# One run of context products per block, beside the 13th of fifteen tiled products, in a two-layer graph-attention kernel

## The chip, the cores and the metric

The kernel runs on one core of a Trainium2 chip. The metric is the device time of one execution in microseconds (us), the median of three. TensorE (PE in the profile; PEld for its weight loads) multiplies, VectorE (DVE), ScalarE (ACT) and GpSimd (POOL) work on tiles, SyncE (SP) issues the transfers. All data is fp32.

## The reference, cut to what matters

There are 128 batches of 64 rows by 768 features, with an adjacency matrix each. The input is normalised and clipped at zero, then two layers follow, and the input is added to their result:

```
m_left, m_right = h @ W_left[l].T, h @ W_right[l].T
u_left, u_right = h @ m_left^T / sqrt(768), h @ m_right^T / sqrt(768)
u   = u_left on and above the diagonal of adj, u_right below it
att = exp(u) * adj / sum over the row
ctx = att @ (h @ W_lin[l].T + b_lin[l])
h   = relu((ctx - mean) / (std + 0.001) * a + b)
```

Here `std` is the deviation with 767 in the divisor. `ctx` is the context.

## The kernel before, in words

**Tiling.** The batches are cut into 16 blocks of 512 rows (`NB = 16`, `T = 512`). Each layer has two passes over the blocks. `pass_one` normalises and transposes the rows, projects them with W_left and then W_right (`project`), and makes the attention (`scores` and a chain of small operations). `pass_two` multiplies with W_lin (`linear`), multiplies with the attention (`context`), and normalises (`finish`). `ps_aux` is two tiles of two PSUM banks each; the four other banks are called X, Y, Z and V.

**Fifteen tiled products.** A 768-wide projection is not done in plain form. It is a bilinear scheme over tiles of 2x128 by 256: 15 products (the list `ORDER`) of sums of weight tiles (`W_SUMS`, on slots named by numbers) with sums of token tiles (`T_SUMS`, tiles `ts`; `B0` to `B5` are raw tiles of `ht`). Each product accumulates into X, Y, Z or V, and after it the bank is read into the result `hl` or `m` with the signs in `ORDER`'s last column (`read`). The first read of a result is an ACT copy (L200), the later ones are DVE additions (L155). A bank is not cleared between most products: the next product in the same bank adds on top, so it may start only when all reads of the product before it in that bank are done. `FIRST` lists the six products that begin a bank anew; `fresh` then fills the bank with a bias on ACT (L605). In index order the banks are X Z X Y X V X Y X V X Y V Z V. The reads after products 0, 2, 4, 6 and 7 are on ACT alone, product 1 has one on each engine, and all others are on DVE; products 8 and 10 have two.

**Order.** Nothing is scheduled by a planner: every engine runs its instructions in the order in which the program writes them. `put(slot, f)` hangs extra work into a block: slot 2i is in the middle of product i, slot 2i+1 behind it and behind its reads. What stands at slot 30 or more when a block ends is carried into the next block with 30 taken off. `idle` holds work without a slot.

**Context and finish.** In `pass_two` the context of block u-1 is made inside block u in two halves, r = 0 after product 0 and r = 1 after product 7 (`ends`). A half is eight matmuls of 64 rows by 64 columns with 384 elements each, over four quadrants of the array, into the two `ps_aux` tiles (L636). `finish` then squares and sums on ACT (L705, L707), takes the inverse on DVE (L710, L711) and scales (`scaled`). In layer 0 the scaling is an ACT copy (L723) and the rows go to DRAM. In layer 1 it is a DVE operation that reads PSUM (L715), then POOL adds the offset row (L718), then DVE adds the residual row from SBUF (`done`, L730) and the result is stored:

```
nc.gpsimd.tensor_add(zs[k], zs[k], rows["b"])
nc.vector.scalar_tensor_tensor(xs[k], zs[k], 0.0, xs[k], op0=ALU.max, op1=ALU.add)
```

The last block of each layer is done in two half-width runs.

**Start.** The first block's rows and the weights of layer 0 are loaded raw, and the weight sums are made by POOL and DVE while the first products run. `hold` makes POOL wait for a tile, so that its sums start late enough. `needs` says which sums DVE makes ahead of which product.

Of the kernel before, what the change touches and what calls it, by code (L numbers as in the profile page):

```python
# [10 lines left out]
F32 = mybir.dt.float32  # L11
# [6 lines left out]
def kernel(  # L18
# [68 lines left out]
    def run(slot):  # L87
# [3 lines left out]
        elif idle:  # L91
            f = idle.popleft()
            if f is not None:
# [3 lines left out]
    SRC = {"l": w_left, "r": w_right, "n": w_lin}  # L97
    RAW = {9: (2, 1), 8: (0, 1), 13: (2, 0), 12: (1, 1), 3: (0, 2), 10: (1, 2), 11: (0, 0), 6: (1, 0), 14: (2, 2)}
    W_SUMS = ((9, "+", 9, 8), (5, "+", 8, 13), (8, "+", 8, 12), (0, "+", 8, 13), (4, "+", 3, 10),
              (11, "+", 11, 13), (1, "+", 4, 11), (7, "+", 6, 10), (6, "-", 12, 6), (12, "-", 14, 12),  # L100
              (12, "-", 12, 9), (6, "+", 6, 5), (2, "-", 9, 14), (10, "-", 14, 10), (10, "-", 10, 9),
              (3, "+", 3, 11), (7, "+", 7, 3))
# [5 lines left out]

    ORDER = ((8, "X", "ta", "+2"), (5, "Z", "u1", "-0+2"), (0, "X", "u2", "+3"), (1, "Y", "u3", "-3"),
             (12, "X", "B3", "-5"), (6, "V", "B0", "-2"), (2, "X", "td", "-4"), (4, "Y", "tb", "+1"),  # L110
             (10, "X", "B4", "+0-2"), (7, "V", "B1", "+3"), (3, "X", "u0", "+1-3"), (11, "Y", "te", "+0"),
             (13, "V", "tc", "-1"), (9, "Z", "tg", "+4"), (14, "V", "tf", "+5"))
    FIRST = {0: ("X", 8), 1: ("Z", 5), 3: ("Y", 1), 5: ("V", 6), 9: ("V", 7), 12: ("V", 13)}
    W = {}
# [98 lines left out]

    ident = const.tile([P, P], F32, name="ident")
    make_identity(nc, ident)
    eps_in = const.tile([P, 1], F32, name="eps_in")
# [3 lines left out]

    diff = const.tile([P, S], I32, name="diff")
    tri = const.tile([P, 2, S], F32, name="tri")
    for h in range(PAIR):
        r = slice(h * S, (h + 1) * S)
        nc.gpsimd.iota(diff[r], pattern=[[-1, S]], base=0, channel_multiplier=1)
    nc.vector.tensor_scalar(tri[:, 0, :], diff, 0.0, None, op0=ALU.is_le)
    nc.vector.tensor_scalar(tri[:, 1, :], diff, 0.0, None, op0=ALU.is_gt)
    def mean_var(mv, halves):
        st = stat.tile([P, 2, 6], F32, name="st")
        for n in range(2):  # L230
            nc.vector.bn_stats(st[:, n, :], halves[n])
        nc.vector.bn_aggr(mv, st)


    XR, KEEP = {}, {}

# [35 lines left out]
    def transpose_rows(l, u, pool):  # L272
# [58 lines left out]
        if (l, u) == (0, 0):  # L331
            ht = HT[key] = big.tile([P, C, T], F32, name="ht")

            def turn(n, q):

                if n < 2:
                    p = ps_aux.tile([P, 2, T], F32, name="aux")
                    banks = [p[:, 0], p[:, 1]]
                else:
                    banks = [ps_st.tile([P, 2 * TH], F32, name=m) for m in ("XY", "ZV")[n - 2]]  # L340
                for m, p in enumerate(banks):
                    for c in range(3):
                        nc.tensor.transpose(p[:, c * P:(c + 1) * P],
                                            xr[q][:, (3 * m + c) * P:(3 * m + c + 1) * P], ident)
                for m, p in enumerate(banks):
                    to = ht[:, 3 * m:3 * m + 3].rearrange("p c (a g s) -> p g c a s", a=4, g=2)
                    to = to[:, q // 2, :, q % 2 * 2:q % 2 * 2 + 2, :]
                    (nc.vector.tensor_copy if n < 2 else nc.scalar.copy)(
                        to, p[:, :3 * P].rearrange("p (c a s) -> p c a s", c=3, a=2))
# [28 lines left out]
    def pass_one(l, aside):  # L378
        with tc.tile_pool(name=f"one{l}", bufs=2, reuse_waits="tile") as sp:
# [110 lines left out]
            just = {}  # L490
            if l == 0:
                load_rows(0, 0, sp)
                warm = stat.tile([P, 1], F32, name="warm", bufs=1)
                nc.scalar.activation(warm, eps_in, AF.Sqrt)
                for f in load_w(0, "l") + load_w(0, "r"):
                    f()
# [14 lines left out]
                hold(KEEP["nb"][:, START[-1]:START[-1] + 1])  # L511
                for f in ws[:3]:
                    f()
                t, w = deque(sums_t((1, 0, 0), nc.vector)), deque([vs[4], vs[3]] + vs[5:])
                needs = ("tw", "wt", "t", "ttww", "wwww", "w", "tw", "t", "ww", "ww", "", "t", "t", "t", "t")
                for i, what in enumerate(needs):
# [14 lines left out]
            for u in range(NB):  # L531
                slot = 0
                if u == 0:
                    if l == 0:
                        rs = sums_w(0, "r", nc.gpsimd)
                        put(16, lambda: hold(M[0][:, 0, 4, 0, :1]))
                        for n in range(0, len(rs), 3):
                            put(17 + n // 3, *rs[n:n + 3])
                    slot = 14 if l else 15
# [69 lines left out]
    def pass_two(l, aside):  # L609
        last = l == L - 1  # L610
        with tc.tile_pool(name=f"two{l}", bufs=2, reuse_waits="tile") as sp:
# [3 lines left out]
            else:  # L615
                places(sp, {"hl": ([P, Q, H], 2), "at": ([P, Q, S], 3), "x": ([P, 2, H], 2),
                            "xb": ([P, H // 32, Q, 32], 1), "z": ([P, H], 3)}, ("hl", "at", "x", "xb", "z"))
            AT, HL = {}, {}

            def load(u):  # L620
                if (2, l, u) not in HT:
                    load_h(2, l, u)
                AT[u] = sp.tile([P, Q, S], F32, name="at", bufs=3)
                nc.sync.dma_start(AT[u], ATT[l][u])

            def context(u, r):
# [5 lines left out]
                for n in range(2):  # L632
                    for (j, k, i) in ((lo, 0, lo), (hi, 0, hi), (lo, 1, hi), (hi, 1, lo)):
# [3 lines left out]
                                         start=True, stop=True)  # L637
                return [c[:, :, :HH] for c in cx]

            def batch(r, k, h):  # L640
# [23 lines left out]
            def finish_last(u, r):  # L664
# [6 lines left out]
                xs = XS[u, r]  # L671
                ss = [stat.tile([P, 1], F32, name="ss_e", bufs=2) for _ in range(2)]
                rs = [stat.tile([P, 1], F32, name="sd_e", bufs=2) for _ in range(2)]
                for k in (1, 0):
# [13 lines left out]
            def residual(u, r):  # L688
                XS[u, r] = [sp.tile([P, H], F32, name="xr", bufs=4) for _ in range(2)]
                for k in range(2):  # L690
                    for h in range(PAIR):
                        nc.sync.dma_start(XS[u, r][k][h * S:(h + 1) * S], x[u * NBB + batch(r, k, h)])

            def finish(u, r):

                cx = context(u, r)
                zs = [sp.tile([P, H], F32, name="z", bufs=4 if last else 3) for _ in range(2)]
                if last and not u and not r:
                    residual(u, r)
                two = "p (n d) -> p n d"  # L700
                ss = stat.tile([P, 2], F32, name="ss")
                sd = stat.tile([P, 2], F32, name="sd1")
                rs = stat.tile([P, 2], F32, name="rs1")
                for k in range(2):
# [8 lines left out]
                def scaled(k):  # L713
# [8 lines left out]
                    else:  # L722
                        nc.scalar.activation(zs[k].rearrange(two, n=2), cx[k], AF.Copy, scale=rs[:, k:k + 1])  # L723
                    for h in range(PAIR):
                        nc.sync.dma_start(ROWS[u][batch(r, k, h)], zs[k][h * S:(h + 1) * S])

                def done(k):
                    if last:
                        xs = XS[u, r]
                        nc.vector.scalar_tensor_tensor(xs[k], zs[k], 0.0, xs[k], op0=ALU.max, op1=ALU.add)  # L730
                        for h in range(PAIR):
                            nc.sync.dma_start(out[u * NBB + batch(r, k, h)], xs[k][h * S:(h + 1) * S])
                        if k and u + r < NB - 1:
                            residual(u + r, 1 - r)

                return [inverse] + [lambda k=k: scaled(k) for k in range(2)] + [lambda k=k: done(k) for k in range(2)]

            def linear(u, rs, base, ends, more):
# [7 lines left out]
                for i, (s, at, t, _) in enumerate(ORDER):  # L746
# [12 lines left out]
                    if i in early:  # L759
                        bank[FIRST[early[i]][0]] = fresh(l, early[i], rs)  # L760
                    if i == 11 and more:
                        AHEAD.append(fresh(l, 0, more))
                    if i in ends:
                        what, slots = ends[i]
                        for f, n in zip(finish(*what), slots):
                            put(n, f)
                    run(base + 2 * i + 1)

            load(0)
            for u in range(NB):  # L770
                turn = not last and u >= NB - 2
                if u + 1 < NB:
                    load(u + 1)
                    put_all(9 if u else 15, affine(2, l, u + 1))
# [6 lines left out]
                    ends = {}  # L781
                    if u:
                        ends = {0: ((u - 1, 0), (6, 7, 8, 11, 12)), 7: ((u - 1, 1), (20, 21, 22, 30, 30))}
                    linear(u, (0, 1), 0, ends, (0, 1) if u + 2 < NB else (0,))
                    for n in sorted(plan):
                        plan[n - 30] = plan.pop(n)
                else:
                    if turn:
                        load_h(1, 1, 0)
                        put_all(28, affine(1, 1, 0), 3)  # L790
                        put_sums_t((1, 1, 0), 38, 2, 30)
                        ends = ({0: ((u - 1, 0), (12, 13, 15, 19, 21)), 11: ((u - 1, 1), (34, 35, 36, 42, 44))},
                                {4: ((u, 0), (50, 51, 52, 56, 58))})
                    else:
                        last_block(u)
                        ends = ({0: ((u - 1, 0), (12, 13, 15, 19, 21)), 9: ((u - 1, 1), (28, 29, 30, 39, 41))},
                                {2: ((u, 0), (44, 45, 47, 61, 62))})
                    linear(u, (0,), 0, ends[0], (1,))
# [53 lines left out]
```

## Time and profile before

| What | Before |
| --- | --- |
| time, median of 3 runs | 2761.18 us (2760.8 to 2761.21) |
| span of the profiled execution | 2761.9 us |
| PE busy | 2731.4 us, 99% |
| DVE busy | 1338.4 us, 48% |
| POOL busy | 1196.8 us, 43% |
| ACT busy | 842.5 us, 31% |
| transfers | 310.80 MB, mean 113 GB/s |
| TensorE clock granted | 0.999 |

A line of the timeline has the start, the duration, the engine, the source line, the operation, what it writes and reads, the shape and how many instructions are merged; in brackets stands how long the engine had been idle and who ended the wait. "issue" means that the profile shows nothing that was waited for. The kernel has two layers of about 55.7 us per block in the first pass and 29.2 us per block in the second.

### The profile page before, as it was taken

How to read it: one execution, taken by the hardware profiler on the slowest of the kernel's cores; microseconds unless marked ns; L12 is line 12 of the kernel's file. 1: busy time of each engine (PE TensorE's matmuls, PEld its weight loads, DVE VectorE, ACT ScalarE, POOL GpSimd, SP SyncE). 2: the span in 40 equal slices, each digit the busy share in tenths (PEclk: the TensorE clock that was granted, in tenths of full speed). 3: DMA queues.
4: the chain of work that ended last, by engine and by line, in shares of the span. 5: the costliest groups of instructions: out<-in, count | busy, mean ns of one | idle time of the engine just before them, and what ended most of it. 6: DMA issues, size and time to landing. Idle time of an engine off the chain costs nothing.

```text
span 2761.9 us, 46187 instructions
## 1 busy us (share of the span) xinstructions
PE 2731.4 (99%) x18712; PEld 2337.1 (85%) x18712; DVE 1338.4 (48%) x2250; ACT 842.5 (31%) x1469; POOL 1196.8 (43%) x940
## 2 busy tenths in 40 slices
PE   8999999999999999999999999999999999999998
PEld 6888888888888888888788888888888888888886
DVE  6555445545453332333335444444444335676667
ACT  3222223222321244444521211121121214444443
POOL 4332442223223465565432344223222325887885
PEclk9999999999999999999999999999999999999999
DMA  6423433343232343443555422443234204555655
GB/s 196 127 75 98 122 80 81 93 122 85 75 85 67 95 136 107 123 142 104 151 127 154 101 75 76 107 119 79 75 98 120 59 26 147 163 168 163 178 162 139
DMA packets 234068, 310.80 MB, mean 113 GB/s; under 512 B 54144, under 2 KB 184448, under 8 KB 225664
## 3 DMA queue, kind: packets, MB, share of 16 engines
q1 hardware_dynamic: 233696, 307.45, 40.4%
q8 instruction: 149, 2.44, 0.4%
q14 instruction: 63, 0.52, 0.1%
q10 hardware_dynamic: 160, 0.39, 0.0%
HBM read 202.91 MB, written 104.86 MB: 111 GB/s over the span
## 4 chain that ended last, share of the span: by engine, by line
PE 96%; DVE 2%; ACT 0%; issue 0%; DMA 0%; SPq 0%; DVEq 0%; ACTq 0%
PE X L422 24%; PE V L422 16%; PE Y L422 12%; PE X L752 12%; PE Z L422 8%; PE V L752 8%; PE Y L752 6%; PE aux L449 5%; PE Z L752 4%; PE aux L636 3%; DVE ts L155 0%; DVE wm L463 0%; DVE m L155 0%; DMA x<-in_x_dram 0%; DVE w_l L155 0%
## 5 line engine op out<-in xcount | busy, mean ns | idle before, releaser
L155 POOL TENSOR_TENSOR ts<-ht 128x512 f32<-128x512 f32 x441 | 585.6, 1339 | 1220.2 <-DMA ht<-h 531.5
L200 ACT ACTIVATE m<-X 128x512 f32<-128x512 f32 (+1 forms) x256 | 151.6, 592 | 1100.5 <-PE X L422 583.3
L155 POOL TENSOR_TENSOR ts<-ht,ts 128x512 f32<-128x512 f32 x189 | 249.1, 1325 | 151.0 <-PE X L752 75.9
L155 DVE TENSOR_TENSOR m<-m,V 128x512 f32<-128x512 f32 (+1 forms) x256 | 173.2, 677 | 269.6 <-PE V L422 269.5
L155 DVE TENSOR_TENSOR m<-m,X 128x512 f32<-128x512 f32 (+1 forms) x256 | 162.8, 677 | 249.1 <-PE X L422 248.4
L752 PE MATMUL X<-w_n,ts 128*128 128x256 f32 x1024 | 244.0, 380 | 1.3 <-DVE hl L155 0.7
L422 PE MATMUL X<-ts,w_l 128*128 128x256 f32 x1024 | 242.8, 380 | 1.7 <-POOL w_l L155 1.1
L422 PE MATMUL X<-ts,w_r 128*128 128x252 f32 (+1 forms) x1024 | 238.8, 376 | 0.0
L155 DVE TENSOR_TENSOR m<-m,Z 128x512 f32<-128x512 f32 (+1 forms) x128 | 87.4, 683 | 306.4 <-ACT m L200 247.3
L422 PEld LDWEIGHTS X<-ts,w_l 128*128 128x128 f32 x1024 | 192.0, 190 | 32.2 <-DVE m L155 2.7
L752 PEld LDWEIGHTS X<-w_n,ts 128*128 128x128 f32 x1024 | 191.6, 190 | 32.5 <-issue 2.1
L422 PEld LDWEIGHTS X<-ts,w_r 128*128 128x128 f32 x1024 | 192.0, 190 | 26.0
L268 ACT ACTIVATE ht<-ht,b_col,a_col 128x512 f32<-128x512 f32 x192 | 143.5, 804 | 133.4 <-DMA ht<-h 133.4
L752 PE MATMUL Y<-w_n,ts 128*128 128x256 f32 x768 | 182.5, 379 | 0.0
L422 PE MATMUL Y<-ts,w_l 128*128 128x256 f32 x768 | 181.4, 379 | 0.0
L200 ACT ACTIVATE hl<-X 128x512 f32<-128x512 f32 (+1 forms) x136 | 77.7, 571 | 333.2 <-PE X L752 330.2
L422 PE MATMUL Y<-ts,w_r 128*128 128x252 f32 (+1 forms) x768 | 179.1, 376 | 0.0
L752 PEld LDWEIGHTS Y<-w_n,ts 128*128 128x128 f32 x768 | 145.8, 190 | 20.4 <-issue 0.6
L422 PEld LDWEIGHTS Y<-ts,w_l 128*128 128x128 f32 x768 | 145.9, 190 | 19.8
L422 PEld LDWEIGHTS Y<-ts,w_r 128*128 128x128 f32 x768 | 145.9, 190 | 17.4
L155 DVE TENSOR_TENSOR hl<-hl,X 128x512 f32<-128x512 f32 (+1 forms) x136 | 83.0, 652 | 145.4 <-PE X L752 140.5
L155 DVE TENSOR_TENSOR hl<-hl,V 128x512 f32<-128x512 f32 (+1 forms) x136 | 89.0, 654 | 128.0 <-PE V L752 127.6
(142 smaller groups left out, 4711.4 us busy)
## 6 DMA issues: line engine op xcount, KB each, us to landing
ht<-h SPq DMA_DIRECT2D x63, 1536.0 KB, 7.3
h<-xb SPq DMA_DIRECT2D x124, 384.0 KB, 6.0
z<-z SPq DMA_DIRECT2D x128, 192.0 KB, 2.9
x<-z SPq DMA_DIRECT2D x128, 192.0 KB, 8.3
x<-in_x_dram SPq DMA_DIRECT2D x120, 192.0 KB, 8.5
xr<-in_x_dram SPq DMA_DIRECT2D x120, 192.0 KB, 3.6
out_dram<-xr SPq DMA_DIRECT2D x120, 192.0 KB, 2.6
adj<-in_adj_dram SPq DMA_DIRECT2D x64, 128.0 KB, 2.7
```

Of the source, the lines that this page charges most:

```text
L155: (eng.tensor_add if sign == "+" else eng.tensor_sub)(o, a, b)
L200: nc.scalar.activation(to(o), p, AF.Copy, scale=1.0 if sign == "+" else -1.0)
L268: nc.scalar.activation(ht, ht, AF.Relu, bias=cols[1][:, c:c + 1], scale=cols[0][:, c:c + 1])
L422: nc.tensor.matmul(p[:, g], w[ORDER[i][0]][:, c, g * P:(g + 1) * P], b()[t][:, c, :].rearrange(bs, s=S)[:, :, :ns], start=(new and g == c ...
L449: nc.tensor.matmul(p[h * S + e:h * S + e + 32, q, e:e + 95], ht[:, c, b * S + e:b * S + e + 32], mb[:, e:e + 95], start=(c == 0), stop=(c ...
L636: nc.tensor.matmul(cx[k][i, m, :HH], at[j, q, :], hl[j, q, m * HH:(m + 1) * HH], start=True, stop=True)
L752: nc.tensor.matmul(p[:, n], b[t][:, c, r * P:(r + 1) * P], w[s][:, c, :], start=(i in FIRST and i not in PRELOAD and n == c == 0), stop=(c ...
```

## The change

It moves the whole context of a block u-1 (u = 1 to 13) into one run of sixteen matmuls after product 12 of block u (`context_block`). The run needs six banks at once, so it takes both `ps_aux` tiles and the banks X and Y, which are then between their last read and the next block's first use. Each row of 768 is cut into 512 and 256 instead of 384 and 384. DVE copies the parts in X and Y to SBUF, so that the banks come free; squares, inverse, scaling and residual of all four tiles follow at fixed slots, the later ones in the next block (`finish_block`). Blocks 14 and 15 keep halves, at other products. Beside that:

- The two first products change places, and so do their weight sums, so that the first product needs one sum (slot 5 = 8 + 12). POOL makes two sums ahead instead of three.
- A tiny transfer that reads the first row tile is put ahead of the weight loads, so that these are issued after that tile has landed.
- The sums of W_right are held until the last token sum `tf`; four of them go from POOL to DVE.
- Attention tiles are loaded later, residual rows at fixed slots; constants that only the start needs move to a pool that is given back.

```diff
-    ORDER = ((8, "X", "ta", "+2"), (5, "Z", "u1", "-0+2"), (0, "X", "u2", "+3"), (1, "Y", "u3", "-3"),
+    ORDER = ((5, "X", "ta", "+2"), (8, "Z", "u1", "-0+2"), (0, "X", "u2", "+3"), (1, "Y", "u3", "-3"),
...
+                nc.sync.dma_start(dram.tile([1, 8], F32, name="first"), XR[0, 0][START[0]][:1, :8])
...
-                for f in ws[:3]:
+                for f in ws[:2]:
...
-                        put(16, lambda: hold(M[0][:, 0, 4, 0, :1]))
-                        for n in range(0, len(rs), 3):
-                            put(17 + n // 3, *rs[n:n + 3])
+                        put(24, lambda: hold(TS[1, 0, 0]["tf"][:, 0, :1]))
+                        put(25, *rs[:7])
+                        put_all(31, rv[7:11])
+                        put(35, *rs[11:14])
+                        put(36, *rs[14:])
...
+            def context_block(u):
...
+                aux = [ps_aux.tile([P, 2, T], F32, name="aux") for _ in range(2)]
+                x, y = (ps_st.tile([P, 2 * TH], F32, name=n) for n in "XY")
+                wide = {(1, 0): y, (1, 1): x, (0, 0): aux[0][:, 0], (0, 1): aux[0][:, 1]}
+                parts = {}
+                for r in (1, 0):
+                    for k in range(2):
+                        parts[r, k] = [wide[r, k], aux[1][:, k, r * D:(r + 1) * D]]
+                    rows_at = ((lo, 0, lo), (hi, 0, hi), (lo, 1, hi), (hi, 1, lo))
+                    first = [(j, k, i, int(j == hi)) for j, k, i in rows_at]
+                    then = [(j, k, i, int(j == lo)) for j, k, i in rows_at[1::2] + rows_at[::2]]
+                    for j, k, i, n in first + then:
+                        q = r + 2 * k
+                        nc.tensor.matmul(parts[r, k][n][i], at[j, q, :], hl[j, q, n * T:T + n * D],
+                                         start=True, stop=True)
...
+            def finish_block(u, more):
...
+                for t in ((1, 1), (1, 0)):
+                    nc.vector.tensor_copy(zs[t][:, cut[0]], parts[t][0])
+                    parts[t][0] = zs[t][:, cut[0]]
...
+                put_each((25, 26, 28, 29), squares)
+                put(30, deviation)
+                put(32, inverse)
+                put_each((33, 34, 35, 36), scaled)
+                if last:
+                    put_each((37, 39, 41, 43), lambda t: added_to(u, *t, zs[t]))
...
-                    if u:
-                        ends = {0: ((u - 1, 0), (6, 7, 8, 11, 12)), 7: ((u - 1, 1), (20, 21, 22, 30, 30))}
+                    if 0 < u < NB - 2:
+                        ends = {12: (u - 1, None)}
+                    elif u:
+                        ends = {5: ((u - 1, 0), (16, 17, 18, 24, 26)), 11: ((u - 1, 1), (28, 29, 30, 37, 39))}
...
-                        ends = ({0: ((u - 1, 0), (12, 13, 15, 19, 21)), 9: ((u - 1, 1), (28, 29, 30, 39, 41))},
-                                {2: ((u, 0), (44, 45, 47, 61, 62))})
+                        ends = ({1: ((u - 1, 0), (13, 14, 16, 20, 22)), 9: ((u - 1, 1), (28, 29, 30, 39, 41))},
+                                {2: ((u, 0), (44, 48, 51, 61, 62))})
```

## The prediction

> **What bounds the kernel now.** I read the page first (busy shares, chain that ended last), then the timeline of PE's weight loads in the second pass of layer 0, then the same stretch of layer 1 on all engines, then the start.
>
> ```profile
> PE 2731.4 (99%) x18712; PEld 2337.1 (85%) x18712; DVE 1338.4 (48%) x2250; ACT 842.5 (31%) x1469; POOL 1196.8 (43%) x940
> ...
> PE 96%; DVE 2%; ACT 0%; issue 0%; DMA 0%; SPq 0%; DVEq 0%; ACTq 0%
> ```
>
> PE never rests, so only two things can move the time: PE's own work, and new waits of PE. The weight loads show what a half context costs (layer 0):
>
> ```profile
> 1011.71 1.70 PEld L752 LDWEIGHTS Y<-w_n,ts 128*128 128x128 f32 x8
> 1013.75 0.21 PEld L636 LDWEIGHTS aux<-hl,at 64*64 64x64 f32 x8 [0.33 <-issue]
> 1014.12 0.15 PEld L636 LDWEIGHTS aux<-hl,at 64*64 64x64 f32 x4 [0.17 <-issue]
> 1014.45 0.15 PEld L636 LDWEIGHTS aux<-hl,at 64*64 64x64 f32 x4 [0.17 <-issue]
> 1015.20 1.59 PEld L752 LDWEIGHTS X<-w_n,ht 128*128 128x128 f32 x8 [0.60 <-issue]
> 1016.82 1.70 PEld L752 LDWEIGHTS V<-w_n,ht 128*128 128x128 f32 x8
> ```
>
> Products follow each other at 1.726 us (1020.27 to 1022.00 and on). Here Y to the context takes 2.04 (0.31 too much), the context 1.45, the next product 1.62 (0.10 less). A half costs 0.31 + 1.45 - 0.10 = 1.66, of which four waves of matmuls, 0.32 apart, are 1.28. So 0.37 is the price of going in and out. In layer 1 a block looks like this:
>
> ```profile
> 2491.17 1.94 DVE L715 SCALAR_TENSOR_TENSOR z<-aux,rs,a 128x768 f32<-128x768 f32 x2
> 2492.26 3.60 POOL L718 TENSOR_TENSOR z<-z,b 128x768 f32<-128x768 f32 x2 [3.77 <-DVE z L715]
> 2494.02 0.69 DVE L155 TENSOR_TENSOR hl<-hl,V 128x512 f32<-128x512 f32 x1 [0.91 <-PE V L752]
> 2494.62 4.00 DVE L730 SCALAR_TENSOR_TENSOR xr<-z,xr 128x768 f32<-128x768 f32 x2
> 2495.81 3.94 POOL L155 TENSOR_TENSOR ts<-ht 128x512 f32<-128x512 f32 x2
> 2500.85 1.28 DVE L155 TENSOR_TENSOR hl<-hl,X 128x512 f32<-128x512 f32 x2 [2.22 <-PE X L752]
> ```
>
> L730 takes 2.0 us, not its own 0.95: DVE waits until POOL's operation is over (2495.86), works 0.82, and POOL's next starts then. They alternate. DVE still has 2.22 us to spare before the two reads of product 8, for which product 10 waits (both in X). The groups by line say that this is so in all blocks:
>
> ```profile
> L730 DVE SCALAR_TENSOR_TENSOR xr<-z,xr x60: 946/2025/2555, 2320.1 to 2741.7; 128x768 f32<-128x768 f32 x60
> ...
> L718 POOL TENSOR_TENSOR z<-z,b x62: 1804/1817/1832, 2318.3 to 2745.9; 128x768 f32<-128x768 f32 x62
> ...
> L715 DVE SCALAR_TENSOR_TENSOR z<-aux,rs,a x62: 1005/1009/1018, 2316.0 to 2744.5; 128x768 f32<-128x768 f32 x62
> ```
>
> L715 reads PSUM and is never stretched. The start:
>
> ```profile
> 7.89 1.02 DVE L231 BATCH_NORM_STATS2 st<-x 128x6 f32<-128x384 f32 x2 [1.40 <-DMA x<-in_x_dram]
> ...
> 11.56 4.18 POOL L155 TENSOR_TENSOR w_l<-w_l,w_l 128x512 f32<-128x512 f32 x3
> ...
> 15.79 1.59 PEld L422 LDWEIGHTS X<-ts,w_l 128*128 128x128 f32 x8 [1.49 <-POOL w_l L155]
> ...
> 24.37 1.59 PEld L422 LDWEIGHTS X<-ht,w_l 128*128 128x128 f32 x8 [1.78 <-issue]
> ...
> 32.38 13.04 POOL L155 TENSOR_TENSOR w_r<-w_r,w_r 128x512 f32<-128x512 f32 x9
> ...
> 43.51 1.59 PEld L422 LDWEIGHTS V<-ts,w_l 128*128 128x128 f32 x8 [1.83 <-DVE m L155]
> ```
>
> **What the Trainium skill says.** "TensorEngine Tiling (Array Packing)", Key Properties: a change of tiling mode drains TensorE, and tiles work independently. The trace agrees: 0.33 us idle going in, and four quadrants running side by side. "SBUF — State Buffer", Who interferes with whom: a DVE operation with two SBUF inputs contends with a GpSimd operation that reads SBUF, one with at most one SBUF input does not. The trace agrees: L730 0.946 alone, 2.025 beside POOL; L715 1.009 always.
>
> **The change part by part.**
>
> *Context runs.* Thirteen blocks in each layer have one run in place of two. The elements are the same: per quadrant 512 + 256 for each half of the rows, 2 x 768 in all. A quadrant does not wait for its neighbours (skill, above), and the order gives those that had 256 their 512 first, so I cost the matmuls at the same 2 x 1.28. One way in and out is saved: 26 x 0.35 = **-9.1 us** (0.37 less a little for the longer run). X and Y are free: product 10's reads end about 2 us before product 12 does, product 11's about 0.8. DVE then copies X and Y (0.68 each by its PSUM reads) while products 13 and 14 (3.45 us) run; the bias copy (0.59) into X is ready about 3 us before the next block needs it. ACT's squares (eight pieces, about 3.9 us by 0.60 and 0.38 for 512 and 256) and the root end before product 0 does; product 0's read comes in time. No PE wait there.
>
> *Layer 0, scaling on ACT.* Four tiles at about 0.94 (L723 is 0.89 in one piece) at slots 3 to 6. Two of them stand before product 2's read: 0.2 + 0.5 + 1.9 + 0.6 = 3.2 us after product 1, and product 4 starts at 3.45. Hidden, by 0.2 only.
>
> *Layer 1, scaling, offset and residual of four tiles at slots 3 to 13.* Before, two tiles at a time were spread over a block; now all four stand ahead of product 8's reads in DVE's queue, and all four POOL additions run together. I write the queue out, in us after product 2's first matmul. DVE: read of product 1 behind ACT's, 0.83 to 1.43; four scalings at 0.95 (0.60 + 0.33 for the pieces) to 5.2; read of product 3 to 5.8. POOL starts the first addition at 2.5, is held to 2.95 by a scaling that has two SBUF inputs (the X and Y parts were copied), and ends the first two at 4.75 and 6.5. Then they alternate: residual (1,1) 6.5 to 7.35, POOL's third to 9.1, residual (1,0) to 9.95, POOL's fourth to 11.7 with DVE's read of product 5 beside it, residual (0,0) to 12.55, then POOL's first token sum of the next block (queued, 1.2) to 13.75, residual (0,1) to 14.6. Now come the two reads of product 8, to 15.85. Product 10 would start at 8 x 1.726 = 13.8, so PE waits **2.0 us**. Bounds: 0.8 if no token sum comes between the last two residuals; 2.6 if POOL starts half a us later. It returns in blocks 2 to 13; in block 14 a half context lies between and leaves 0.4. 12 x 2.0 + 0.4 = **+24.4 us**. Bounds +10 and +32.
>
> *Start.* Row three's statistics waited 1.40 us for a landing, as weight loads shared the bandwidth. With the weights behind the first row, rows three and four should land about 2 us earlier; DVE's chain then gains 1.25. The first product waited for three POOL sums (4.18); with one it waits for `ta`, about 13.0 instead of 15.79. But by product 4 DVE must make ten sums instead of nine, so 1.5 us are left at 24.37. The 1.83 and 0.31 us of waits near 43.51 came while POOL's W_right sums stretched DVE's; holding those sums back takes that away. In return seven sums (9.1 to 10.1 us) from about 38.3 end at 47.4 to 48.4, and product 3 of the right projection wants the seventh at 47.0: 0.4 to 1.4 given back. Net **-2.5 us** (-1 to -4).
>
> *The rest at nothing.* The 512/256 cut costs DVE and ACT 0.1 us per tile, counted above. The changed loads are hidden: attention and residual rows come half a block before use. In the two half-width blocks of each layer the slots move both ways: one wait for `ps_aux` (DVE's scaling of block 13 stands before it), and one wait of about 1 us near the end relieved by the later slots 48 and 51. Zero, within 1.5.
>
> Sum: 2761.2 - 9.1 - 2.5 + 24.4 = **2774.0 us**.
>
> **The rivals.**
> *A. No new wait in layer 1*: 2761.2 - 9.1 - 2.5 = 2749.6. For it: DVE is only 48% busy, and without the lock its queue would reach product 8's reads at 9.8, with 2.6 us in hand. Against: the alternation shows in 59 of the 60 L730 (one took 0.946).
> *B. A short wait of 0.8*: about 10 us over the layer, 2760: no change. It needs POOL's queue empty once per block.
> *C. The unequal pieces don't overlap*: waves as long as their longest member, 4 x 0.43 per half instead of 4 x 0.32, so +0.86 per block, 26 x 0.86 = +22.4. Without the DVE wait 2772, with it about 2796. Against: before, a quadrant held back by a semaphore in the last half context of layer 0 didn't stop its three neighbours.
>
> **How the numbers follow.** Forecast 0.56, A 0.29, B 0.10, C 0.05. Slower: forecast and C, 0.61, less 0.02 for its low end. Faster: A and a little of B, 0.31. Same (2755.7 to 2766.7): 0.10. The range must hold A and the forecast with their bounds: A less 2.5 is 2747, the forecast with waits of 2.6 is 2782.
>
> **What would show it.** A block of layer 0's second pass should take 28.84 us, not 29.2. In layer 1 PE should wait about 2 us before product 10, the last in X, ended by DVE's `hl`, with L730 at 2.0 to 2.6 us at slots 7 to 13; a block then takes 30.9. If that wait is missing, A holds. If the context run is longer than 2.8 us, C holds. The first product should start near 13 us. The forecast is wrong if DVE gets to product 8's reads before the product has ended.

## The result and the profile after

| What | Before | After |
| --- | --- | --- |
| time, median of 4 runs each | 2760.99 us (2760.46 to 2761.21) | 2781.11 us (2780.51 to 2781.36) |
| span of the profiled execution | 2761.9 us | 2779.5 us |

The kernel is slower: the ratio is 1.0073, with a 95% interval of 1.0055 to 1.009, which is +20.1 us. The prediction had 2774.0, and a range from 2747 to 2783, so the time lies near the range's upper end.

The page after, first the busy times of the engines, then the chain that ended last, then one of the costliest groups (count, after the bar busy us and mean ns, then the engine's idle time just before and who ended most of it):

```profile
PE 2727.2 (98%) x18712; PEld 2348.4 (84%) x18712; DVE 1365.4 (49%) x2333; ACT 855.8 (31%) x1703; POOL 1196.3 (43%) x935
...
PE 89%; DVE 7%; issue 1%; DMA 1%; POOL 1%; ACT 1%; SPq 0%; DVEq 0%; ACTq 0%; POOLq 0%
...
L842 PE MATMUL X<-w_n,ts 128*128 128x256 f32 x1024 | 245.7, 381 | 21.7 <-DVE hl L155 20.5
```

PE's busy time fell by 4.2 us while the span grew by 17.6, so PE now waits. DVE's share of the chain went from 2% to 7%, although its share of busy time hardly moved. The last line says which wait it is: products into bank X of the second pass, ended by a DVE read of `hl`.

A table by stretch, made from the starts of weight loads and the end of the span, says where it lies (us):

| Stretch | Before | After | Difference |
| --- | --- | --- | --- |
| start of the span to layer 0's second pass | 913.27 | 913.27 | 0 |
| layer 0, second pass, blocks 0 to 14 | 405.88 | 401.22 | -4.7 |
| to layer 1 | 65.07 | 64.93 | -0.1 |
| layer 1, first pass | 895.78 | 894.14 | -1.6 |
| layer 1, second pass, blocks 0 to 14 | 405.92 | 425.61 | +19.7 |
| blocks 14 and 15, to the end of the span | 75.99 | 80.35 | +4.4 |

The rows add up to the +17.6 of the spans; the other 2.5 of the medians' difference are not in these two executions.

**The context run.** The weight loads of layer 0's second pass, after:

```profile
1018.42 1.27 PEld L842 LDWEIGHTS V<-w_n,ts 128*128 128x128 f32 x6
1020.02 0.13 PEld L670 LDWEIGHTS Y<-hl,at 64*64 64x64 f32 x1 [0.33 <-issue]
...
1022.22 0.15 PEld L670 LDWEIGHTS aux<-hl,at 64*64 64x64 f32 x2 [0.27 <-issue]
1022.76 1.59 PEld L842 LDWEIGHTS Z<-w_n,ts 128*128 128x128 f32 x8 [0.39 <-POOL w_l L155]
```

From the first load of the context to the next product's first are 2.74 us, where two halves took 2 x 1.45. The block takes 28.84 us.

**The wait in layer 1.** The timeline of a block in the middle of layer 1, cut to DVE, POOL and the product that waits:

```profile
2457.11 0.69 DVE L155 TENSOR_TENSOR hl<-hl,Z 128x512 f32<-128x512 f32 x1 [2.58 <-ACT hl L200]
...
2458.94 9.02 POOL L768 TENSOR_TENSOR z<-z,b 128x768 f32<-128x768 f32 x4 [6.61 <-DVE z L763]
...
2461.93 0.68 DVE L155 TENSOR_TENSOR hl<-hl,Y 128x512 f32<-128x512 f32 x1
...
2462.52 3.75 DVE L788 SCALAR_TENSOR_TENSOR xr<-z,xr 128x768 f32<-128x768 f32 x2
...
2466.20 0.68 DVE L155 TENSOR_TENSOR hl<-hl,V 128x512 f32<-128x512 f32 x1
...
2466.80 3.92 DVE L788 SCALAR_TENSOR_TENSOR xr<-z,xr 128x768 f32<-128x768 f32 x2
...
2467.91 3.94 POOL L155 TENSOR_TENSOR ts<-ht 128x512 f32<-128x512 f32 x2
...
2470.64 1.27 DVE L155 TENSOR_TENSOR hl<-hl,X 128x512 f32<-128x512 f32 x2
2471.97 1.99 PE L842 MATMUL X<-w_n,ts 128*128 128x256 f32 x8 [1.71 <-DVE hl L155]
```

Read it from the bottom. Product 10 starts when DVE's two reads of product 8 end, at 2471.91. In front of them DVE was never idle from 2461.93 on: two pairs of residuals and two reads fill it. Each pair takes 3.75 or 3.92 us for 2 x 0.95 of work, because POOL's additions and then its token sums run beside it. By the weight loads PE stands still for 2.1 us, 12 times in the layer:

```profile
PEld X L842 <- DVE hl L155: 25.4, 12, 2.1
```

(This is the view of waits, for PE's weight loads, from 2300 to 2700 us: total, times, longest.) POOL pays too. In the view of one line, minimum, median and maximum in ns, the residual is L788 and the addition is L768:

```profile
L788 DVE SCALAR_TENSOR_TENSOR xr<-z,xr x60: 944/1976/2575, 2339.3 to 2759.8; 128x768 f32<-128x768 f32 x60
...
L768 POOL TENSOR_TENSOR z<-z,b x52: 1812/2392/2547, 2335.7 to 2712.0; 128x768 f32<-128x768 f32 x52
```

The residual's median is about what it was before (1976 for 2025 ns); POOL's addition went from 1817 to 2392, since now residuals stand beside it.

**The start.** The beginning of the span after:

```profile
3.88 0.30 SPq L501 DMA_DIRECT2D first<-x  x1
...
7.41 1.02 DVE L235 BATCH_NORM_STATS2 st<-x 128x6 f32<-128x384 f32 x2 [0.92 <-DMA x<-in_x_dram]
...
11.07 2.51 POOL L155 TENSOR_TENSOR w_l<-w_l,w_l 128x512 f32<-128x512 f32 x2
12.68 1.45 DVE L155 TENSOR_TENSOR ts<-ht 128x512 f32<-128x512 f32 x1
...
14.24 1.59 PEld L426 LDWEIGHTS X<-ts,w_l 128*128 128x128 f32 x8 [0.76 <-POOL w_l L155]
```

The tiny transfer holds the weights back as meant (their first load is issued at 4.23 us, before at 2.58), yet the third row's statistics start only 0.48 us earlier (7.41 for 7.89), and the first product 1.55 earlier (14.24 for 15.79). What it waits for is `ta`, which DVE ends at 14.13; POOL's sums, which the last line names, had ended at 13.58.

### The profile page after: what moved, and what is told of

It is laid out like the page before. It is cut to its first block, busy times and chain, and to the rows that moved or that the text cites. A ratio compares the mean times of both kernels' runs of the same rounds, so it can differ in the third digit from the quotient of the medians.

```text
span 2779.5 us, 46460 instructions
## 1 busy us (share of the span) xinstructions
PE 2727.2 (98%) x18712; PEld 2348.4 (84%) x18712; DVE 1365.4 (49%) x2333; ACT 855.8 (31%) x1703; POOL 1196.3 (43%) x935
## 4 chain that ended last, share of the span: by engine, by line
PE 89%; DVE 7%; issue 1%; DMA 1%; POOL 1%; ACT 1%; SPq 0%; DVEq 0%; ACTq 0%; POOLq 0%
PE X L426 23%; PE V L426 16%; PE Y L426 12%; PE X L842 8%; PE Z L426 8%; PE V L842 6%; PE aux L453 5%; PE Y L842 4%; PE Z L842 4%; DVE xr L788 2%; PE aux L670 2%; DVE hl L155 2%; DVE z L763 2%; PE Y L670 1%; DMA out_dram<-xr 1%
## 5 line engine op out<-in xcount | busy, mean ns | idle before, releaser
L155 POOL TENSOR_TENSOR ts<-ht 128x512 f32<-128x512 f32 x441 | 574.7, 1314 | 1224.2 <-DMA ht<-h 563.2
L155 POOL TENSOR_TENSOR ts<-ht,ts 128x512 f32<-128x512 f32 x189 | 239.4, 1274 | 135.1 <-PE X L842 60.6
L768 POOL TENSOR_TENSOR z<-z,b 128x768 f32<-128x768 f32 x52 | 117.2, 2285 | 88.1 <-DVE z L763 88.1
```

The source lines that it names most:

```text
L155: (eng.tensor_add if sign == "+" else eng.tensor_sub)(o, a, b)
L768: nc.gpsimd.tensor_add(zs[t], zs[t], rows["b"])
```

## The experiments

All are compared with the kernel before, run beside them: a median of 2761.80 us for e1 to e4 and 2761.11 us for e5 to e7. Theory 1 in what was expected is the prediction's: in layer 1 DVE comes late to product 8's reads, since its four residuals alternate with POOL's additions.

**e1, no offset.** POOL's addition of `b` (zeros in the inputs) is left out in the runs of layer 1, so that nothing of it alternates with DVE.

```diff
-                    if last:
-                        nc.gpsimd.tensor_add(zs[t], zs[t], rows["b"])
-                    else:
+                    if not last:
                         kept(u, *t, zs[t])
```

> Leaves out POOL's addition of the offset row b in the thirteen context runs of layer 1 (b is a row of zeros in this data, so the values stay). Theory 1 (DVE's residual additions wait for POOL one by one, and the reads of product 8 stand behind them): without the four POOL additions most residuals take 0.95 us, DVE is at product 8's reads before they are due, PE's wait of 2.1 us before product 10 goes, a block takes 28.84 us instead of 30.82, and the time is 2781.1 - 12 x 2.0 = 2757. Theory 2 (DVE's queue of four scalings and four residuals is too long by itself): a wait of over 1 us stays and the time is above 2768.

Measured: 2756.09 us, ratio 0.9981 (0.9974 to 0.9989). Its timeline at the same place of the layer, and one line's instructions, are:

```profile
2456.98 1.82 DVE L786 SCALAR_TENSOR_TENSOR xr<-z,xr 128x768 f32<-128x768 f32 x2
...
2459.32 1.82 DVE L786 SCALAR_TENSOR_TENSOR xr<-z,xr 128x768 f32<-128x768 f32 x2
...
2466.55 1.28 DVE L155 TENSOR_TENSOR hl<-hl,X 128x512 f32<-128x512 f32 x2 [1.04 <-PE X L840]
```

```profile
L786 DVE SCALAR_TENSOR_TENSOR xr<-z,xr x60: 945/950/2558, 2341.6 to 2737.7; 128x768 f32<-128x768 f32 x60
```

The residuals take 0.95 us, DVE waits for product 8 and not product 10 for DVE, and the view of waits for the same stretch (2300 to 2700 us) has no wait for DVE's `hl` any more. The blocks take 28.84 us, as in layer 0: in layer 1 one run per block is worth its 0.36 us as well. But this kernel takes POOL's work away together with the alternation, so it can't tell what the order of DVE's queue costs; e2 keeps the additions.

**e2, the fourth residual later.** One of the four residuals goes behind the reads of product 8, from slot 13 of the next block to slot 17 (43 and 47 less 30); the loads of the next residual rows move behind it.

```diff
-                    put_each((37, 39, 41, 43), lambda t: added_to(u, *t, zs[t]))
+                    put_each((37, 39, 41, 43 if u == NB - 4 else 47), lambda t: added_to(u, *t, zs[t]))
...
-                        for r, slot in enumerate((14, 18)):
+                        for r, slot in enumerate((14, 18) if u == NB - 2 else (18, 20)):
```

> The last of the four residual additions of a run goes from slot 43 to slot 47 (behind product 8's reads; in block 14 it stays), and the loads of the residual rows from slots 14 and 18 to 18 and 20. Theory 1 (the queue ahead of product 8's reads, lengthened by POOL): the reads come 2.0 us earlier, a wait of 0 to 0.3 us is left, a block takes about 28.9 to 29.1, time 2757 to 2760. Theory 3 (PE waits for something else, the bias copy into V or POOL's token sums): the wait moves but stays, 2775 or more.

Measured: 2758.30 us, ratio 0.9987 (0.998 to 0.9994), some 23 us below the kernel after (-3.6 us against before, where that one has +20.1). The waits of PE's weight loads from 2300 to 2700 us:

```profile
PEld Z L842 <- POOL ts L155: 5.1, 13, 0.4
PEld X L842 <- DVE hl L155: 1.9, 11, 0.2
```

The wait for `hl` is 0.2 us per block where it was 2.1, and blocks take 28.87. The residual's median is 1976 ns as in the kernel after, and the addition's 2392. So the alternation itself did not go away; it stopped mattering when one residual stood behind the deadline.

**e3, runs in layer 0 alone.** Layer 1 as before the change; layer 0 and the start as after it.

```diff
-                    if 0 < u < NB - 2:
+                    if last and u:
+                        ends = {0: ((u - 1, 0), (6, 7, 8, 11, 12)), 7: ((u - 1, 1), (20, 21, 22, 30, 30))}
+                    elif 0 < u < NB - 2:
                         ends = {12: (u - 1, None)}
...
```

(The residual loads and the slots of layer 1's last two blocks go back as well.)

> Layer 1 as before the change (two halves per block, residual loads behind the residual additions, its last blocks too), layer 0 and the start as changed. Theory 1: no wait in layer 1, 13 x 0.36 = 4.7 us saved in layer 0, start +0.5: 2761.0 - 4.2 = 2757. Theory 4 (a context run costs as much as two halves in either layer): 2761.

Measured: 2756.59 us, ratio 0.9984 (0.9976 to 0.9991), -4.4 us by the ratio (-6.6 to -2.5). Its second pass of layer 0 takes 401.22 us for blocks 0 to 14, as after; layer 1's blocks take 29.20 and its last two together 75.76, both as before. The whole loss of the kernel after lies in layer 1.

**e4, the start alone.** Halves in both layers; only the start is changed (as e3, with `if u:` in the first line added, and layer 0's last block as before; attention tiles are still loaded later).

> Both layers with halves as before the change; only the start is changed (order of the first two products and of the weight sums, the small transfer ahead of the weight loads, the W_right sums held). The prediction's sum says -2.5 us: 2758.5. What the trace of the changed kernel shows up to block 6 says +0.5 us: 2761.5. The difference to the run with layer 0 changed is the worth of the thirteen runs of layer 0: 4.7 us by theory 1.

Measured: 2761.49 us, ratio 1.0001 (0.9992 to 1.0009, which is -2.2 to +2.5 us): no change can be measured. The difference to e3, 4.9 us, is what layer 0's runs are worth, for 4.7 expected. In its trace layer 0's second pass starts 2.29 us earlier than before (910.98), and layer 1's first pass, which no edit touches, takes 4.07 more. Of these, 3.78 are two waits in block 1, for ACT, which itself had waited until 1468.7 us for rows `ht` to land. That stretch was 893.8 to 899.9 us in the traces of these kernels, so a single trace cannot tell what a gain of 2 us ahead of it is worth.

**e5, later residual, and one run fewer at the end.** e2, and the changeover from runs to halves comes one block earlier in layer 1, with the residual rows loaded earlier and the last block's slots as before the change.

```diff
+                    if last and u == NB - 3:
+                        ends = {5: ((u - 1, 0), (15, 15, 16, 27, 28)), 9: ((u - 1, 1), (24, 25, 26, 32, 33))}
+                    elif last and u == NB - 2:
+                        ends = {0: ((u - 1, 0), (6, 7, 8, 11, 12)), 7: ((u - 1, 1), (20, 21, 22, 30, 30))}
-                    if 0 < u < NB - 2:
+                    elif 0 < u < NB - 2:
...
```

> Layer 1 keeps its context runs for twelve blocks with the fourth residual addition behind product 8's reads, goes back to halves one block earlier, and takes its last three blocks' slots from before the change. In the changed kernel the stretch from block 14 of layer 1 to the end takes 80.4 us, before 76.0. If the slots of the last blocks are the cause, it takes 76.0 to 77 here, and the time is 4 us less than with the fourth addition moved alone: 2752 to 2754. If the runs ahead of them are the cause, it stays near 80 and the time at 2757.

Measured: 2755.51 us, ratio 0.9979 (0.9972 to 0.9985), 5.6 us below before. This is the lowest median, though its interval overlaps those of all others but e4. It fell between the two values expected. Blocks 14 and 15 take 76.98 us, which speaks for the slots; the last block takes 46.23 of them (46.79 before, 49.81 after, to the end of the span), so its slots did cost it about 3. But what block 14 lost, 30.54 for 29.20, came back in block 13, 30.55, the first with halves behind a run:

```profile
2659.17 1.59 PEld L842 LDWEIGHTS X<-w_n,ts 128*128 128x128 f32 x8 [0.60 <-issue]
2660.79 1.70 PEld L842 LDWEIGHTS Y<-w_n,ts 128*128 128x128 f32 x8
2663.98 1.59 PEld L842 LDWEIGHTS X<-w_n,ht 128*128 128x128 f32 x8 [1.49 <-ACT hl L200]
```

It is the wait that the kernel after has in block 14 (1.48, shown below), one block earlier, so this cost moved with the changeover. Block 14 took 30.75 here, mostly because its first half context waits 1.37 us in the middle for DVE's `hl`.

**e6, W_right sums early.** e3, with the start of these sums as before the change: three per slot from slot 17 on, behind the first result instead of `tf`, and all on POOL again.

```diff
-                        put(24, lambda: hold(TS[1, 0, 0]["tf"][:, 0, :1]))
-                        put(25, *rs[:7])
-                        put_all(31, rv[7:11])
-                        put(35, *rs[11:14])
-                        put(36, *rs[14:])
+                        put(16, lambda: hold(M[0][:, 0, 4, 0, :1]))
+                        for n in range(0, len(rs), 3):
+                            put(17 + n // 3, *rs[n:n + 3])
```

> As the kernel with runs in layer 0 only, but the W_right sums start at slot 16 on POOL alone, as before the change. If holding them back is what frees DVE in the left projection and costs the right one, then the waits before products 13 and 14 of the left projection return (2.1 us) and those before products 3 and 4 of the right one (2.4 us) go: the second block starts within 0.5 us of where it did. If the hold pays, the second block starts 2 us later.

Measured: 2756.75 us, ratio 0.9985 (0.9979 to 0.9992). Against e3 block 0's left projection is 1.50 longer (29.92 for 28.42) and its right one 2.18 shorter (25.50 for 27.68). Holding the sums, with four of them on DVE, gives 1.5 and takes 2.2, which is 0.7 on the wrong side, too little for the medians to show. The second block starts 0.89 us earlier than in e3 (69.13 for 70.02; 0.21 of it were there at the first product), which is neither of the two values expected.

**e7, W_right sums split otherwise.** e3, with DVE making the fifth to seventh sums and POOL taking two of DVE's later ones, so that product 3's sum would come in time.

```diff
-                        put(25, *rs[:7])
-                        put_all(31, rv[7:11])
+                        put(25, *rs[:4], *rs[7:9])
+                        put_all(28, rv[4:7])
+                        put_all(33, rv[9:11])
```

> As the kernel with runs in layer 0 only, but of the W_right sums DVE makes the fifth to seventh (from slot 28) and POOL the eighth and ninth. If the seventh sum's place in POOL's queue is what delays product 3 of the right projection, the waits of 1.7 and 0.7 us before products 3 and 4 fall to under 1 us together and the second block starts 1.5 us earlier. If DVE's sums wait for POOL one by one, as its residual additions do, the gain is under 0.7 us.

Measured: 2757.41 us, ratio 0.9986 (0.9979 to 0.9994): the gain hoped for did not come. Its timeline in the right projection of block 0:

```profile
43.38 2.36 DVE L155 TENSOR_TENSOR w_r<-w_r,w_r 128x512 f32<-128x512 f32 x2
...
47.46 1.68 PEld L426 LDWEIGHTS Y<-ts,w_r 128*128 128x128 f32 x8
...
50.96 0.85 DVE L155 TENSOR_TENSOR w_r<-w_r,w_r 128x512 f32<-128x512 f32 x1
...
51.92 3.02 PEld L426 LDWEIGHTS X<-ht,w_r 128*128 128x128 f32 x8 [2.79 <-issue]
```

Product 3 (Y) no longer waits, but product 4 waits 2.79 us for its own sum, which DVE ends at 51.81 (the line itself names no cause), and the projection takes 29.64, 1.96 more than in e3. Two sums that DVE makes beside POOL take 2.36 us, and one more takes 1.30; at the start, where POOL is idle, one takes 0.68. Moving sums between these two engines moved the wait.

## Why the prediction was right, point by point

The direction and its cause were right, and the time was 7.1 us above the forecast, since two terms of the sum were mis-sized: the start and the last two blocks. By its own steps:

**The context runs (-9.1): right.** Layer 0 gained 4.66 us over the 13 blocks that have a run, 0.36 each for the forecast 0.35, and e1 shows the same 28.84 us in layer 1. Rival C falls with the 2.74 us of a run: the pieces of 512 and 256 overlap between quadrants. This is what the Trainium skill, "TensorEngine Tiling (Array Packing)", Key Properties, says of independent tiles.

**The margin of 0.2 us in layer 0: held.** No wait of PE for ACT's scaling shows in these 13 blocks.

**The wait in layer 1 (12 x 2.0): right, in size and in mechanism.** The blocks take 30.82 in place of e1's 28.84, 1.98 more. The forecast's queue can be laid on the fence of the result, with product 2's first matmul at 2456.28: read of product 3 done at 6.3 (forecast 5.8, as the four scalings took 4.3 us for 3.8, a delay that DVE's waiting for POOL took up), the second residual at 10.0 (9.95), the fourth POOL addition at 11.7 (11.7), DVE's fourth residual at 14.4 (14.6), its reads of product 8 done at 15.6 (15.85). POOL's token sum did come between the last two residuals; that is why rival B's 0.8 did not happen. Rival A needed DVE and POOL not to alternate, and e1, where they do not, comes nearest to it: 5.7 us below before by the medians. A had 11.6; less the 2.5 of the start and less the 3.6 that e1's trace loses in its last two blocks (79.62 for 75.98), that is 5.5. e2 adds that not the alternation alone makes the wait but alternation ahead of a deadline. The Trainium skill, "SBUF — State Buffer", Who interferes with whom, says that issue order, not the shape of the operation, decides who blocks; here both engines keep a queue, and both lose: DVE's residual goes from 0.95 to 1.98, POOL's addition from 1.82 to 2.39.

**The start (-2.5): mis-sized.** By the first scores of block 0 the gain was 0.73 us (71.93 for 72.66), and by layer 0's second pass nothing. e1 to e5 have the same start, and with the kernel after their traces show what a single one hides: the gain at the first scores is 0.6 to 1.75 us, and the second pass starts between 910.98 and 914.05 (before 913.27). e4's interval, -2.2 to +2.5 us, just excludes -2.5, but not the -1 at the end of the forecast's own range. Two terms were off. "Rows three and four should land about 2 us earlier": the third row's statistics came 0.5 earlier here and 0.5 to 1.45 in the six traces, so the first product started at 14.24 (13.28 to 14.24) and not near 13. And the sums of W_right that are held back cost more than the 0.4 to 1.4 given for them. The timeline after, in the right projection of block 0:

```profile
39.11 14.39 POOL L155 TENSOR_TENSOR w_r<-w_r,w_r 128x512 f32<-128x512 f32 x10
...
48.95 1.57 PEld L426 LDWEIGHTS Y<-ts,w_r 128*128 128x128 f32 x8 [1.70 <-POOL w_r L155]
...
51.25 1.57 PEld L426 LDWEIGHTS X<-ht,w_r 128*128 128x128 f32 x8 [0.72 <-issue]
```

The forecast had POOL begin at 38.3 and PE need the seventh sum at 47.0. POOL began at 39.11, since `tf` ended there, and PE waited 1.70 us before product 3 and 0.72 before product 4. Against e6 these waits cost 2.2 us, and the balance of the hold is +0.7. Block 1 then lost the 0.7 us again, and more: the kernel after waits 1.62 us in the middle of a product behind the first scores, for which the profile names no cause (its later blocks made up the rest):

```profile
75.99 0.73 PEld L426 LDWEIGHTS Z<-ts,w_l 128*128 128x128 f32 x4
78.34 0.83 PEld L426 LDWEIGHTS Z<-ts,w_l 128*128 128x128 f32 x4 [1.62 <-issue]
```

All six traces with this start have it, 0.80 us (e4) to 1.71 (e1), and so has e6 with 0.90; before and e7, which come later to the first scores, have not. The transfers of instructions in the traces (`q8 instruction` on the page: 149, one per 18.7 us on average) point to a cause: one of them landed at 76.99, and the wait ended 1.35 us later. In the nine traces, the 35 waits of over 0.44 us without a named cause that fall in scores all end 1.2 to 1.6 us after such a landing. That PE then waited for its own instructions is read from these times alone, and no run tests it.

**The last two blocks of layer 1 ("a half context lies between and leaves 0.4", and "zero, within 1.5"): mis-sized, +4.4.** This is most of what was missing. Block 14 lost 1.34, and not to DVE's reads of product 8:

```profile
2712.91 0.81 ACT L801 ACTIVATE z<-aux 128x768 f32<-128x768 f32 x1 [0.62 <-DVE xr L788]
...
2714.05 1.50 ACT L272 ACTIVATE ht<-ht,b_col,a_col 128x512 f32<-128x512 f32 x2
2715.46 0.57 ACT L200 ACTIVATE hl<-X 128x512 f32<-128x512 f32 x1
...
2716.08 1.59 PEld L842 LDWEIGHTS X<-w_n,ht 128*128 128x128 f32 x8 [1.48 <-ACT hl L200]
```

Product 8 waits for ACT's read of product 6, for 1.48 us. In front of that read stand the squares of the half context, the second of which waited 0.62 us until a residual of the run before had let go of its tile, and the scaling of the next block's rows. e1, where the residuals aren't late, bears this out: the second square doesn't wait, PE's wait is 0.75 us, and block 14 takes 29.81, so about half of the 1.34 comes from the late residual and the rest from ACT's order. The prediction followed DVE's queue through this block, not ACT's. Block 15 lost 3.0, by the weight loads after:

```profile
2732.21 0.20 PEld L645 LDWEIGHTS aux<-hl,at 64*64 64x64 f32 x4 [0.80 <-DVE z L811]
2733.13 0.21 PEld L645 LDWEIGHTS aux<-hl,at 64*64 64x64 f32 x8 [0.73 <-DVE z L811]
...
2741.97 0.73 PEld L842 LDWEIGHTS V<-w_n,ht 128*128 128x128 f32 x4 [1.37 <-ACT V L616]
2743.03 0.20 PEld L645 LDWEIGHTS aux<-hl,at 64*64 64x64 f32 x4 [0.33 <-DVE z L811]
2743.93 0.21 PEld L645 LDWEIGHTS aux<-hl,at 64*64 64x64 f32 x8 [0.71 <-DVE z L811]
```

The contexts wait for DVE's scaling to free `ps_aux`; the prediction named one such wait and set a relieved one against it, but there are three of 0.7 to 0.8 us and one of 1.37 for a bias copy. Before, the contexts of this block waited 0.33 us each at their start and, but for 0.38 in the last one of either kernel, not in between. The relief came, but smaller than the 1 us given: the wait near the end went from 1.07 to 0.45. With last-block slots as before, e5 has 46.23 there.

**The sum.** -4.7 and -4.7 for the runs, 0 for the start, +23.8 for the waits and +4.4 at the end make +18.8; the forecast with its two mis-sized terms put right, 2774.0 + 2.5 + 4.0, is 2780.5. No step names the -1.6 of layer 1's first pass, the +0.6 of the block behind it (27.07 for 26.46) and the -0.1 ahead of it; with them the sum is +17.7, and the spans differ by 17.6. Of the -1.6, 1.0 are shorter waits without a named cause in the scores (6.87 for 7.88) and 0.6 is another such wait at the start of the pass (0.24 for 0.88). The pass varies by some 6 us between traces. One bound was summed wrongly: by the terms given, waits of 2.6 make 2781.2 and not 2782, which changes nothing.

## What to carry to other kernels

An engine that is busy for half of the span can still hold up the bound engine: write out its queue in order between two deadlines, with the stretched durations, and see what stands ahead of the deadline. If too much does, moving one operation behind it may be enough; here one residual out of four, 4 slots later, was worth some 23 us. Do this for every engine that has a read before a deadline, at the changeover between two schedules above all, where the tail of one and the head of the other meet in the same queue.

## What the runs showed of the hardware

Two engines that contend did not starve one another when both had work queued: DVE's and POOL's operations took turns, and each lasted about as long as itself and more than half of one of the other's. DVE's residual had a median of 1.98 us for 0.95 alone (1.25 to 2.58 for nearly all of the 60), and POOL's addition 2.39 for 1.82. In 64x64 mode, pieces of unequal length cost no more than equal ones: sixteen matmuls of 512 and 256 columns in one run took 2.74 us, where two runs of eight with 384 took 1.45 each. PE's waits of 0.44 us and more without a named cause in or just behind the scores, dense runs of small matmuls, ended 1.2 to 1.6 us after a transfer of instructions had landed.
